# Band sums in two row halves behind the scores, the next query product behind them, and five of eight band groups normalized earlier

## The chip, the cores and the metric

The kernel runs on one core of a Trainium2 chip. The metric is device microseconds (us) of one execution, lower is better; before the change the median of three runs is 2634.23 us (2633.81 to 2636.1).

A core has five engines that run side by side and meet through semaphores: TensorE (PE in the profile; PEld is its weight load), VectorE (DVE), ScalarE (ACT), GpSimd (POOL) and SyncE (SP, which here issues transfers). Each engine takes its instructions in the order in which the program lists them. Matmuls write to PSUM, eight banks of 512 fp32 columns on 128 partitions.

## The reference

One layer over x of shape (2, 256, 128, 128), that is B, T, F, C, all fp32: attention along T with a causal mask, attention along F with a band mask, then a feed-forward layer, each with a layer norm before it and a residual after it.

```python
cm = _causal_mask(x.shape[1])
bm = _band_mask(x.shape[2], BAND)          # |i - j| <= 16 of 128
xt = _ln(x, ln_t_w, ln_t_b).transpose(0, 2, 1, 3)
x = x + _mha(xt, t_wi, ..., H_T, cm).transpose(0, 2, 1, 3)
xf = _ln(x, ln_f_w, ln_f_b)
x = x + _mha(xf, f_wi, ..., H_F, bm)       # 4 heads of 32
xn = _ln(x, ln_n_w, ln_n_b)
h = jax.nn.gelu(xn @ w1.T + b1, approximate=False)   # 128 -> 512 -> 128
x = x + (h @ w2.T + b2)
```

## The kernel before, in words

The work is cut into groups of 512 tokens (`NT` = 4 tiles of 128). First come 128 groups of attention over time (`OverTime`), which end some 930 us into the program. Then follow 16 runs; each has 8 groups of band attention (`OverBands`) and then the 8 feed-forward groups (`FeedForward`) on the same tokens. Everything is unrolled, and every instruction on the main path is kept in program order (`InOrder`, whose one line, L907, is the line of nearly all rows of the profile). So the order in which `run` (L1275) calls the groups' methods is the order on each engine.

`run` is a pipeline: in step n it works on group n and its neighbours. In the steps of a run I count the band groups 0 to 7, and call "step n" the one whose scores are those of band group n. There, before the change, TensorE does in this order:

- scores of n: per tile and half of the keys, 4 heads, 64 keys by 80 queries (only queries that can lie in the band);
- sums of n-1: for each head the column sums of the weights, as a product of a block of ones with all 128 keys, 512 queries;
- weigh of n-1: values times weights; output of n-2: the out projection;
- queries, keys, then values of n+1.

ScalarE does in the step: exponentials of the four heads of n (`pf`), logarithm and exponential that make a first inverse of the sums of n-1 (`ln`, `r`), then copies of queries, keys and values of n+1 (`qT`, `kT`, `v`). VectorE does: clamp and band of the fourth head of n (`bank<-bank,band`), normalization and transposition of group n+3 (`xh`, `z`; the result goes to DRAM as `turned` and comes back as `xnT`), the residual of n-2 (`x<-bank,x`, which empties the out projection's bank), and a correction step of the inverse with the division of n-1 (`bank<-bank,r`, `u`, `oT`). In some steps it also does the layer norm's statistics of a later group (`stats`, `mv`). GpSimd masks the other three heads (`pf<-pf`, six instructions) and makes the roots (`rstd`).

The last steps of a band run overlap with the first feed-forward steps. A feed-forward step is two hidden products, the second product of the group before (`w2T_sb,hT`, 64 products of 128 columns), and two more hidden products.

PSUM banks are handed out in rotation (`turn_of_bank`, L943): a product that is written to a bank waits until the reader of the bank's last content is done.

## Time and profile before

| what | value |
|---|---|
| median of 3 runs | 2634.23 us |
| span of the profiled execution | 2631.9 us |
| PE busy | 2617.8 us (99%) |
| DVE busy | 2140.8 us (81%) |
| ACT busy | 1838.8 us (70%) |
| POOL busy | 1958.6 us (74%) |
| in a stretch of band steps (1459.70 to 1507.00): PE, DVE, ACT, POOL | 47.30, 40.81, 38.22, 31.45 of 47.30 us |
| in the feed-forward steps behind it (1507.00 to 1565.50) | 58.50, 44.46, 25.16, 38.43 of 58.50 us |

The span goes from the first to the last instruction of one profiled execution; its own total time is not given apart from that, and the span stands 2.3 us under the median of the runs. In the rows of the timeline a row gives the start, the time from the first start to the last end, the engine, the line, the operation, what it writes and reads, and the count. A fp32 matmul appears as two records. Since matmuls are pipelined, the time of a block on TensorE is read from its start to the start of the next block, not from the second column.

### The profile page before, as it was taken

The numbers are of one execution on the slowest core, as the hardware profiler recorded it, in microseconds if no ns is written. First come the engines' busy times: TensorE is split into PE (matmuls) and PEld (weight loads), VectorE is DVE, ScalarE is ACT, GpSimd is POOL, SyncE is SP. The second block draws the span as 40 slices with busy tenths as digits, with TensorE's granted clock in tenths as the row PEclk, the third lists the DMA queues.
The fourth block names the chain that finished last, engine by engine and source line by source line (L and its number), as shares of the span: only waits on it lengthen the run. The fifth ranks groups of instructions, "written<-read, shape, count | busy, mean of one in ns | idle before, by whom it ended". The sixth has DMA issues, their size and how long they took to land.

```text
span 2631.9 us, 156460 instructions
## 1 busy us (share of the span) xinstructions
PE 2617.8 (99%) x68688; PEld 1837.4 (70%) x68688; DVE 2140.8 (81%) x6410; ACT 1838.8 (70%) x3543; POOL 1958.6 (74%) x2311
## 2 busy tenths in 40 slices
PE   9999999999999999999999999999999999999999
PEld 6666666666766767666777776667676677777776
DVE  8888888888888887977878779788797797887974
ACT  7989988999899875564655746647557466475573
POOL 7999999999999987666667666665776666757762
PEclk9999999999999999999999999999999999999999
DMA  6656555565565454445454544554454445554543
GB/s 155 167 149 158 149 149 149 155 155 149 149 158 149 122 127 119 115 123 127 118 124 124 123 122 117 126 128 120 122 126 120 120 119 131 123 120 123 123 104 88
DMA packets 469797, 344.97 MB, mean 131 GB/s; under 512 B 43120, under 2 KB 404464, under 8 KB 469104
## 3 DMA queue, kind: packets, MB, share of 16 engines
q1 hardware_dynamic: 468408, 334.41, 50.5%
q8 instruction: 540, 8.85, 1.5%
q14 instruction: 153, 1.25, 0.2%
q10 hardware_dynamic: 696, 0.46, 0.1%
HBM read 167.98 MB, written 166.72 MB: 127 GB/s over the span
## 4 chain that ended last, share of the span: by engine, by line
PE 99%; DVE 0%; issue 0%; DMA 0%; ACT 0%; ACTq 0%; DVEq 0%
PE bank L907 99%; DMA x<-in_x 0%; DVE xh L907 0%; DVE bank L907 0%; DVE res L907 0%; DVE stats L907 0%; DVE oT L907 0%; DVE u L907 0%; DVE xnT L907 0%; ACTq L907 0%; ACT p L907 0%; DVE vy L907 0%; ACT lnv L907 0%; DVE mv L907 0%; ACT root L907 0%
## 5 line engine op out<-in xcount | busy, mean ns | idle before, releaser
L907 ACT ACTIVATE hT<-bank,b 128x512 f32<-128x512 f32 x512 | 348.1, 688 | 524.2 <-PE bank L907 483.2
L907 POOL TENSOR_SCALAR_AFFINE_SELECT pf<-pf 128x512 f32<-128x512 f32 x768 | 477.7, 637 | 185.3 <-ACT pf L907 159.1
L907 PEld LDWEIGHTS bank<-w2T_sb,hT 128*32 128x32 f32 x16384 | 467.4, 110 | 54.8 <-issue 29.0
L907 PE MATMUL bank<-xnT,wf 128*32 128x512 f32 x4096 | 492.4, 592 | 0.5 <-DVE xnT L907 0.5
L907 PE MATMUL bank<-xnT,w1f 128*32 128x512 f32 x4096 | 486.3, 592 | 0.2 <-issue 0.2
L907 PE MATMUL bank<-w2T_sb,hT 128*32 128x128 f32 x16384 | 482.8, 273 | 1.0 <-issue 1.0
L907 ACT ACTIVATE p<-bank 128x512 f32<-128x512 f32 (+1 forms) x1024 | 430.6, 494 | 62.9 <-PE bank L907 62.9
L907 DVE TENSOR_SCALAR xh<-x,mv,rstd 128x160 f32<-128x160 f32 (+1 forms) x1012 | 394.3, 432 | 59.7 <-POOL rstd L907 49.4
L907 POOL TENSOR_SCALAR_AFFINE_SELECT p<-p 128x1024 f32<-128x1024 f32 (+2 forms) x384 | 364.5, 949 | 57.5 <-ACT p L907 49.1
L907 PEld LDWEIGHTS bank<-wf,xnT 128*32 128x32 f32 x8192 | 243.3, 110 | 144.1 <-issue 101.6
L907 POOL TENSOR_TENSOR p<-p,p 128x512 f32<-128x512 f32 x256 | 324.6, 1291 | 10.6
L907 DVE BATCH_NORM_STATS2 stats<-x 128x6 f32<-128x128 f32 x1536 | 329.0, 276 | 3.4 <-DMA x<-in_x 3.4
L907 POOL TENSOR_SCALAR rstd<-mv 128x4 f32<-128x4 f32 x251 | 57.8, 230 | 361.7 <-DVE mv L907 360.5
L907 PEld LDWEIGHTS bank<-xnT,w1f 128*32 128x32 f32 x4096 | 183.6, 110 | 171.6 <-issue 109.6
L907 PE MATMUL bank<-qT,kT 32*64 32x80 f32 (+4 forms) x16384 | 302.0, 271 | 0.1
L907 PEld LDWEIGHTS bank<-qT,kT 32*64 32x64 f32 x16384 | 260.0, 131 | 51.2 <-ACT kT L907 50.6
L907 DVE TENSOR_TENSOR res<-bank,res 128x512 f32<-128x512 f32 (+1 forms) x259 | 170.3, 658 | 153.3 <-PE bank L907 144.7
L907 ACT ACTIVATE pf<-bank 128x512 f32<-128x512 f32 x512 | 265.8, 602 | 35.5 <-PE bank L907 31.3
L907 PE MATMUL bank<-wn,oT 128*32 128x128 f32 x8192 | 283.8, 274 | 0.1
L907 DVE STREAM_TRANSPOSE z<-xh 128x512 f32<-128x512 f32 x380 | 270.3, 711 | 13.3
L907 PE MATMUL bank<-wf,xnT 128*32 128x128 f32 x8192 | 276.5, 273 | 0.0
L907 POOL TENSOR_TENSOR rstd<-rstd,mhalf 128x4 f32<-128x4 f32 x251 | 260.8, 1039 | 20.9
(100 smaller groups left out, 3820.3 us busy)
## 6 DMA issues: line engine op xcount, KB each, us to landing
turned<-z SPq DMA_DIRECT2D x1520, 64.0 KB, 2.7
xnT<-turned SPq DMA_DIRECT2D x380, 256.0 KB, 3.2
x<-res SPq DMA_DIRECT2D x256, 128.0 KB, 2.5
x<-x SPq DMA_DIRECT2D x128, 256.0 KB, 4.1
out<-res SPq DMA_DIRECT2D x252, 128.0 KB, 2.3
x<-in_x SPq DMA_DIRECT2D x124, 256.0 KB, 4.3
x<-in_x SPq DMA_DIRECT2D x4, 128.0 KB, 2.8
x<-in_x SPq DMA_DIRECT2D x6, 64.0 KB, 2.9
```

The costliest lines, as they stand in the source:

```text
L907: return self.tc.keep_in_program_order(emit(*args, **kwargs))
```

## The change

- The sums of a band group n-1, in the steps in which n is a band group too, are made in two parts right behind the scores of n. Of 128 queries of a tile, the first 48 can only have weights on the first 64 keys, and the last 48 on the last 64 keys. The outer part sums these over 64 rows each, into two banks (`rp` and `lower`); the middle part sums the 32 queries between over all 128 rows. The logarithm and the first multiplication then work on two pieces.
- The queries' product of n+1 stands right behind the sums, ahead of the weighing; the copy of the queries stands behind the inverse.
- The residual of n-2 stands inside the division of n-1, behind its first multiplication.
- Band groups 3 to 7 of every run but the first are normalized and transposed three steps earlier than before, beside another group: 3, 4 and 5 in the last three feed-forward steps of the run before, 6 and 7 in the steps of bands 0 and 1. Bands 5 to 7 then normalize feed-forward groups as before, bands 2 to 4 nothing.
- Statistics and root of the first feed-forward groups stand behind the masks of their step, statistics on VectorE thus right behind the clamp.
- In feed-forward steps the hidden products of n stand between the halves of the second product of n-1, and the stores of results are issued one step later, from ScalarE's queue.
- Banks are taken from a list in the order in which they were given back.

The diff, cut to its core:

```diff
+EDGE = HALF - BAND
@@ class Attention
-    def divide(self):
+    def divide(self, between=None):
...
-        vector.tensor_tensor(self.rp, self.rp, self.r0, ALU.mult)
+        self.multiply()
+        if between is not None:
+            between()
         u = path.work.tile([P, NT * P], F32, name="u", bufs=2)
         vector.scalar_tensor_tensor(u, self.rp, 2.0, self.r0, ALU.subtract, ALU.mult)
@@ class OverBands
+    def outer_sums(self):
+        self.split = True
+        self.rp = self.take("rp", [P, NT * P])
+        self.lower = self.take("lower", [P, NT * EDGE])
+        for h in range(H):
+            self.sums_of(h, in_tiles(self.rp)[:, :, 0:EDGE], slice(0, EDGE), slice(0, HALF))
+            self.sums_of(h, in_tiles(self.lower), slice(P - EDGE, P), slice(HALF, P))
+
+    def middle_sums(self):
+        q = slice(EDGE, P - EDGE)
+        for h in range(H):
+            self.sums_of(h, in_tiles(self.rp)[:, :, q], q, slice(0, P))
+
+    def sums_of(self, h, to, q, rows):
+        self.path.tensor.matmul(
+            to[rows_of(h)], self.path.k.ones[rows, 0:D], self.p[rows, h, :, q],
+            start=True, stop=True, skip_group_check=True,
+        )
+
+    def invert(self):
...
+        path.scalar.activation(in_tiles(ln)[:, :, 0 : P - EDGE], in_tiles(self.rp)[:, :, 0 : P - EDGE], AF.Ln)
+        path.scalar.activation(in_tiles(ln)[:, :, P - EDGE : P], in_tiles(self.lower), AF.Ln)
...
+    def multiply(self):
...
+        vector.tensor_tensor(rp[:, :, low], in_tiles(self.lower), r0[:, :, low], ALU.mult)
+        self.give("lower")
+        vector.tensor_tensor(rp[:, :, q], rp[:, :, q], r0[:, :, q], ALU.mult)
@@ class FeedForward
+    def weigh_around(self, other):
+        self.zp = self.take("zp", [P, NT, P])
+        self.weigh_tiles(range(0, 2))
+        other.hidden((2,))
+        self.weigh_tiles(range(2, NT))
+        other.hidden((3,))
@@ class BoundedPath
+    def release(self, i):
+        if i in self.free:
+            self.free.remove(i)
+        self.free.append(i)
@@ run
         def statistics_of_feed(n):
-            if n + 5 in early:
-                do(n + 5, "statistics")
             if at(n + 4, FeedForward) and n + 4 not in early:
                 do(n + 4, "statistics", "root")
+        def turn_ahead(n):
+            for i in (n + 3, n + 6):
+                ahead = at(n + 3, OverBands) and at(i, OverBands) and i not in run0
+                if not at(i, OverTime) and (i == n + 3 or ahead) and not at_turn(i):
+                    do(i, "normalize", "turn")
...
-            if n + 4 in early:
-                do(n + 4, "root")
             do(n, "first_half", "first_function", "first_mask")
+            if n + 4 in early:
+                do(n + 4, "statistics", "root")
...
+            self.storing = self.scalar if feeds[2] and n < len(groups) - NT else self.sync
+            do_at(n - 2, FeedForward, "put")
...
-            do_at(n + 3, (OverBands, FeedForward), "normalize", "turn")
+            turn_ahead(n)
...
-            do(n - 1, "weigh")
+            self.two_parts = bands[2]
+            if bands[2]:
+                do(n - 1, "sums")
+            if bands[2] and bands[3]:
+                do(n + 1, "queries")
+            if feeds[1] and feeds[2]:
+                groups[n - 1].weigh_around(groups[n])
+            else:
+                do(n - 1, "weigh")
             do(n - 1, "invert_exactly" if turn else "invert")
+            if bands[2] and bands[3]:
+                do(n + 1, "take_query")
...
-            do(n - 1, "divide")
+            if bands[1] and bands[2]:
+                groups[n - 1].keep = True
+                groups[n - 1].divide(partial(do, n - 2, "finish"))
+            else:
+                do(n - 1, "divide")
...
-            do_at(n + 1, OverBands, "queries_keys", "take_query", "take_key")
+            if bands[2] and bands[3]:
+                do(n + 1, "keys", "take_key")
+            else:
+                do_at(n + 1, OverBands, "queries_keys", "take_query", "take_key")
```

Three places in the order of the instructions matter for what follows. A row names what is written and read and the output's shape; the number behind `bank` tells the eight banks apart (108 to 115). The first is TensorE in a band step between the scores of n (`qT,kT`) and those of n+1: sums (`pf,ones`), weigh (`pf,v`), output (`wn`,`oT`), then queries and keys (`xnT,wf`) and values (`wf,xnT`). Before:

```order
L907 MATMUL bank_113<-qT,kT 64x80
L907 MATMUL bank_108<-pf,ones 32x512 x4
L907 MATMUL bank_109<-pf,v 32x128 x16
L907 MATMUL bank_114<-wn_241,oT 32x128 x16
L907 MATMUL bank_115<-xnT,wf_238 32x512 x4
L907 MATMUL bank_110<-xnT,wf_238 32x512 x4
L907 MATMUL bank_111<-wf_238,xnT 32x128 x16
```

and of the change:

```order
L1031 MATMUL bank_115<-pf,ones 32x192
L1031 MATMUL bank_108<-pf,ones 32x4x32 x4
L1031 MATMUL bank_114<-xnT,wf_238 32x512 x4
L1031 MATMUL bank_110<-pf,v 32x128 x16
L1031 MATMUL bank_113<-wn_241,oT 32x128 x16
L1031 MATMUL bank_111<-xnT,wf_238 32x512 x4
L1031 MATMUL bank_109<-wf_238,xnT 32x128 x16
L1031 MATMUL bank_112<-qT,kT 64x80
L1031 MATMUL bank_114<-qT,kT 64x80
L1031 MATMUL bank_115<-qT,kT 64x80
L1031 MATMUL bank_113<-qT,kT 64x80
```

The first row of the change is the last of the eight outer products (four of 32x4x48 into bank 108 alternate with four of 32x192 into bank 115). Queries moved up to stand behind the sums. The last four rows are the four heads' scores of n+1: the fourth head goes to bank 113, into which the out projection of n-2 was written in the same step, and the third to bank 115, which held `lower`.

The second place is VectorE in a band step with statistics. Before, from one clamp to the next:

```order
L907 SCALAR_TENSOR_TENSOR bank_113<-bank_113,band 128x512
L907 TENSOR_SCALAR xh<-x,mv,rstd 128x5x32 x4
L907 STREAM_TRANSPOSE z<-xh 128x512
L907 TENSOR_TENSOR x_27227<-bank_114,x_27227 128x512
L907 TENSOR_TENSOR bank_108<-bank_108,r_29670 128x512
L907 SCALAR_TENSOR_TENSOR u<-bank_108,r_29670 128x512
L907 TENSOR_TENSOR oT<-bank_109,u 128x4x4x32
L907 BN_STATS stats<-x_27227 128x6 x4
L907 BN_AGGR mv<-stats 128x2 x4
```

and of the change, in the steps of bands 5 and 6:

```order
L1031 SCALAR_TENSOR_TENSOR bank_112<-bank_112,band 128x512
L1031 BN_STATS stats<-x_27483 128x6 x4
L1031 BN_AGGR mv<-stats 128x2 x4
L1031 TENSOR_SCALAR xh<-x_27483,mv,rstd 128x5x32 x4
L1031 STREAM_TRANSPOSE z<-xh 128x512
L1031 TENSOR_TENSOR bank_115<-bank_109,r_30151 128x4x48
L1031 TENSOR_TENSOR bank_115<-bank_115,r_30151 128x4x80
L1031 TENSOR_TENSOR x_27483<-bank_113,x_27483 128x512
L1031 SCALAR_TENSOR_TENSOR u<-bank_115,r_30151 128x512
L1031 TENSOR_TENSOR oT<-bank_114,u 128x4x4x32
```

The statistics moved from behind the division to right behind the clamp, and the residual (`x<-bank`) moved behind the two multiplications. Before, the steps of bands 3, 4 and 5 have statistics, and all eight steps have the normalization (`xh`, `z`). Now bands 4, 5 and 6 have statistics and bands 2, 3 and 4 have no normalization, so both meet in the steps of bands 5 and 6.

The third place is ScalarE in a band step, from the last exponential of n to the copy of the values of n+1. Before:

```order
L907 ACTIVATE pf<-bank_115 128x512
L907 ACTIVATE ln<-bank_110 128x512
L907 ACTIVATE r_50758<-ln 128x512
L907 ACTIVATE qT<-bank_109,bq_283 128x512
L907 COPY kT<-bank_112 128x512
L907 COPY v<-bank_113 128x512
```

and of the change:

```order
L1031 ACTIVATE pf<-bank_113 128x512
L1031 ACTIVATE ln<-bank_114 128x4x80
L1031 ACTIVATE ln<-bank_109 128x4x48
L1031 ACTIVATE r_51929<-ln 128x512
L1031 ACTIVATE qT<-bank_111,bq_283 128x512
L1031 COPY kT<-bank_108 128x512
L1031 COPY v<-bank_115 128x512
```

The order of the steps is the same; the logarithm became two instructions. The product that `qT` copies is now ready earlier.

More of the change, by code (lines that the diff above doesn't have):

```diff
@@ L380, in __init__, with take, give @@
         self.before, self.store = before, store
+        self.taken = {}
+    def take(self, name, shape, i=None):
+        free = self.path.free
+        if i is None:
+            i = free[0]
+        if i in free:
+            free.remove(i)
+        self.taken[name] = i
+        return self.path.bank(shape, name, i)
+    def give(self, *names):
+        for name in names:
+            if name in self.taken:
+                self.path.release(self.taken.pop(name))
     def load(self):
@@ L569, in bias, with queries, keys, queries_keys @@
         )
-    def queries_keys(self):
+    def queries(self):
+        path = self.path
+        self.qp = self.take("qp", [P, NT * P], self.place.get("qp"))
+        product(path, self.qp, path.k.wf[self.which][:, 0:P], self.xnT)
+    def keys(self):
         path = self.path
         wf = path.k.wf[self.which]
-        self.qp = path.bank([P, NT * P], "qp", self.place.get("qp", path.held.pop("qp", None)))
-        product(path, self.qp, wf[:, 0:P], self.xnT)
-        self.kp = path.bank([P, NT * P], "kp", self.place.get("kp"))
+        self.kp = self.take("kp", [P, NT * P], self.place.get("kp"))
         product(path, self.kp, wf[:, P : 2 * P], self.xnT)
+    def queries_keys(self):
+        self.queries()
+        self.keys()
     def take_query(self):
@@ L663, in values @@
         wv = path.k.wf[self.which][:, 2 * P : 3 * P]
-        self.vp = [path.bank([P, 2, P], "vp", self.place.get(f"vp{s}")) for s in range(2)]
+        self.vp = [self.take(f"vp{s}", [P, 2, P], self.place.get(f"vp{s}")) for s in range(2)]
         for i in range(NT):
@@ L679, in first_tiles @@
         self.p0 = path.work.tile([P, 2, H, 2 * P], F32, name="p0", tag="p", bufs=3)
-        self.s0 = {h: path.bank([P, 2, 2 * P], "sp", path.banks[f"a{h}"]) for h in range(H)}
+        self.s0 = {h: self.take(f"s0{h}", [P, 2, 2 * P], path.banks[f"a{h}"]) for h in range(H)}
     def second_tiles(self):
@@ L685, in second_tiles @@
         self.p1 = path.work.tile([P, 2, H, 2, P], F32, name="p1", tag="h", bufs=2)
[L686 removed]
+        self.s1 = {h: self.take(f"s1{h}", [P, 2, P], path.banks[f"b{h}"]) for h in range(H)}
     def first_scores(self, h, s, e):
@@ L728, in weigh @@
         path, v = self.path, self.v
-        rp = path.bank([P, 2, 2, P], "rp", self.place.get("rp"))
+        rp = self.take("rp", [P, 2, 2, P], self.place.get("rp"))
         for n in range(2):
@@ L771 @@
     which = 1
-    follow = ("yp",)
     by_vector = 1
+    split = False
+    rp = None
     def scores(self, heads):
         path = self.path
-        self.sp = {h: path.bank([P, NT * P], "sp") for h in heads}
+        self.sp = {h: self.take(f"sp{h}", [P, NT * P]) for h in heads}
         for i in range(NT):
@@ L823, in weigh @@
             )
-        self.op = path.bank([P, NT * P], "op")
+    def weigh(self):
+        path = self.path
+        if self.rp is None:
+            self.sums()
+        self.op = self.take("op", [P, NT * P])
         for i in range(NT):
@@ L867, in second_function, with weigh_tiles @@
         self.gelus((2, 3))
+    def weigh_tiles(self, tiles):
+        path, NI = self.path, self.path.k.NI
+        for i in tiles:
+            for j in range(NI):
+                product(
+                    path, self.zp[:, i], self.hT[:, j, i * P : (i + 1) * P], path.k.w2T[:, j, :],
+                    start=(j == 0), stop=(j == NI - 1),
+                )
+    def weigh_around(self, other):
[4 more added lines that the diff above has]
+        other.hidden((3,))
     def weigh(self):
@@ L871, in weigh @@
         if self.last:
-            zp = [path.bank([P, P], "zp") for i in range(NT)]
+            zp = [self.take(f"zp{i}", [P, P]) for i in range(NT)]
         else:
-            self.zp = path.bank([P, NT, P], "zp")
+            self.zp = self.take("zp", [P, NT, P])
             zp = [self.zp[:, i] for i in range(NT)]
@@ L1288, in do_at @@
                 do(n, *names)
-        for i in range(len(groups) - 2):
-            if at(i, OverBands) and at(i + 1, OverBands):
-                groups[i].follow = ("yp", "qp")
         run0 = [i for i in range(len(groups)) if at(i, OverBands)][: RUN // NT]
@@ L1412, in run @@
                 statistics_of_feed(n)
-            if not turn:
+            if feeds[1] and feeds[2]:
+                do(n, "second_function")
+            elif not turn:
                 do(n, "second_half", "second_function")
```

96 lines of the change are left out of this document (72 added, 24 removed).

## The prediction

> **What bounds the kernel now.** I read the page first, for which engine the end hangs on:
>
> ```profile
> span 2631.9 us, 156460 instructions
> PE 2617.8 (99%) x68688; PEld 1837.4 (70%) x68688; DVE 2140.8 (81%) x6410; ACT 1838.8 (70%) x3543; POOL 1958.6 (74%) x2311
> PE 99%; DVE 0%; issue 0%; DMA 0%; ACT 0%; ACTq 0%; DVEq 0%
> ```
>
> TensorE is busy nearly always and is nearly the whole chain. So time is won by less TensorE work or by fewer hidden pauses, and lost wherever TensorE newly waits. A busy PE can hide pauses, so next I took the timeline and read block starts. One band step, scores to scores:
>
> ```profile
> 1497.43 0.97 PE L907 MATMUL bank<-qT,kT 32*64 32x80 f32 x64
> 1498.33 1.06 PE L907 MATMUL bank<-pf,ones 128*32 128x512 f32 x8
> 1499.21 1.06 PE L907 MATMUL bank<-pf,v 128*32 128x128 f32 x32
> 1500.08 1.06 PE L907 MATMUL bank<-wn,oT 128*32 128x128 f32 x32
> 1500.95 1.90 PE L907 MATMUL bank<-xnT,wf 128*32 128x512 f32 x16
> 1502.67 1.06 PE L907 MATMUL bank<-wf,xnT 128*32 128x128 f32 x32
> 1503.66 0.97 PE L907 MATMUL bank<-qT,kT 32*64 32x80 f32 x64
> ```
>
> A step lasts 6.23 us: scores 0.90, sums 0.88, weigh 0.87, output 0.87, queries and keys 1.72, values 0.99. How much is pause? The starts and ends of runs tell:
>
> ```profile
> 925.92 0.97 PE L907 MATMUL bank<-qT,kT 32*64 32x80 f32 x64
> ...
> 1459.73 0.96 PE L907 MATMUL bank<-qT,kT 32*64 32x80 f32 x64
> 1478.43 0.96 PE L907 MATMUL bank<-qT,kT 32*64 32x80 f32 x64
> 1491.20 0.97 PE L907 MATMUL bank<-qT,kT 32*64 32x80 f32 x64
> 1565.44 0.97 PE L907 MATMUL bank<-qT,kT 32*64 32x80 f32 x64
> 1599.81 0.64 PE L907 MATMUL bank<-pf,v 128*32 128x128 f32 x16 [0.30 <-issue]
> 2624.28 1.49 PE L907 MATMUL bank<-w2T_sb,hT 128*32 128x128 f32 x48
> ```
>
> From the first band scores (925.92) to the end of the last product (2625.77) are 1699.9 us for 16 runs. The run from 1459.73 to 1565.44 took 105.7; two of its steps (1478.43 to 1491.20) took 12.77, 0.31 over twice 6.23, so a clean run is 105.4. All 16 clean would be 1686, so pauses cost some 13.5 us. They look like the row at 1599.81: in the middle of a block, on nobody ("issue").
>
> **The sums.** Eight records of 512 columns, four side by side, take 0.88 us: 0.86 ns a column. The scores are 64 records of 80 columns; one after another they would take 4.4 us, four abreast 1.1, and they take 0.90. So row tiles do run side by side, about eight abreast where none waits. Two parts need two passes of 192 columns (0.33 us, eight abreast) and two of 128 (0.22), together 0.55. But the shape of the tiles changes once more in each step (scores 32 by 64, outer 64 by 32, then 128 by 32). The values' block takes 0.99 against 0.87 for the same 32 records of 128 columns in weigh: 0.12 for a change of shape. I take 0.55 + 0.12 + 0.01 for a slow start = 0.68, a gain of 0.20 a step. Ends: 0.55 if no change costs anything; 1.00 if the two row halves run in turn.
>
> [...]
>
> There are seven such steps a run, bands 1 to 7. Whether TensorE can use the 0.20 is set by what else ends late there.
>
> **The steps of bands 5 and 6: VectorE.** The fourth head's scores of n+1 now go into the bank that the residual of n-2 empties, and VectorE does that residual after everything else up to the multiplication. The prices, from a step with statistics, and from one in which VectorE had waited for the scores:
>
> ```profile
> 1479.58 0.70 DVE L907 SCALAR_TENSOR_TENSOR bank<-bank,band 128x512 f32<-128x512 f32 x1 [0.64 <-PE bank L907]
> ...
> 1486.15 0.67 DVE L907 SCALAR_TENSOR_TENSOR bank<-bank,band 128x512 f32<-128x512 f32 x1
> 1486.73 1.60 DVE L907 TENSOR_SCALAR xh<-x,mv,rstd 128x160 f32<-128x160 f32 x4
> 1488.37 0.71 DVE L907 STREAM_TRANSPOSE z<-xh 128x512 f32<-128x512 f32 x1
> 1489.00 0.65 DVE L907 TENSOR_TENSOR x<-bank,x 128x512 f32<-128x512 f32 x1
> 1489.58 0.69 DVE L907 TENSOR_TENSOR bank<-bank,r 128x512 f32<-128x512 f32 x1
> 1490.30 0.69 DVE L907 SCALAR_TENSOR_TENSOR u<-bank,r 128x512 f32<-128x512 f32 x1
> 1491.02 0.69 DVE L907 TENSOR_TENSOR oT<-bank,u 128x512 f32<-128x512 f32 x1
> 1491.63 0.86 DVE L907 BATCH_NORM_STATS2 stats<-x 128x6 f32<-128x128 f32 x4
> 1492.41 0.36 DVE L907 BATCH_NORM_AGGREGATE mv<-stats 128x2 f32<-128x6 f32 x4
> 1492.69 0.67 DVE L907 SCALAR_TENSOR_TENSOR bank<-bank,band 128x512 f32<-128x512 f32 x1
> ```
>
> The clamp can start 1.15 us after the scores (1479.58 less 1478.43). This step kept VectorE busy for 6.54 us, more than TensorE's 6.23; before, the excess fell on later work. In the new order, from the start of the scores: 1.15, clamp 0.58, statistics 1.06, normalization 1.64, transposition 0.63, so 5.06. Then two multiplications in place of one. The prices of whole and half:
>
> ```profile
> L907 DVE TENSOR_TENSOR bank<-bank,r 128x512 f32<-128x512 f32 x240 | 166.8, 695 | 102.1 <-PE bank L907 78.9 <-ACT r L907 23.2
> L907 DVE TENSOR_TENSOR orow<-bank,rows_sb 128x256 f32<-128x256 f32 x1 | 0.4, 423 | 0.0
> ```
>
> That is 1.06 ns a column and 0.15 fixed, so 0.36 and 0.49 for 192 and 320 columns; with handovers 0.90. The residual takes 0.65: its end is at 6.61, and TensorE goes on at about 6.65, though it could at 6.03. The rest of VectorE's step (0.72, 0.61) delays the next clamp by 0.07, so step 6 lasts 6.72. Against 6.23 before: +0.42 and +0.49. Nothing covers this: behind the fourth head stand the whole sums, queries and weighing. Ends: no loss at all, if something lets the residual go earlier; 0.1 more each if handovers add up.
>
> **Step 1, and the chain of the other steps: ScalarE.** In the step of band 1 there is no output product, and ScalarE runs without a pause:
>
> ```profile
> 1466.85 0.97 PE L907 MATMUL bank<-qT,kT 32*64 32x80 f32 x64
> 1467.86 2.07 ACT L907 ACTIVATE pf<-bank 128x512 f32<-128x512 f32 x4 [0.29 <-PE bank L907]
> 1469.79 0.63 ACT L907 ACTIVATE ln<-bank 128x512 f32<-128x512 f32 x1
> 1470.45 0.63 ACT L907 ACTIVATE r<-ln 128x512 f32<-128x512 f32 x1
> 1470.99 0.67 ACT L907 ACTIVATE qT<-bank,bq 128x512 f32<-128x512 f32 x1
> 1471.11 0.70 DVE L907 TENSOR_TENSOR bank<-bank,r 128x512 f32<-128x512 f32 x1 [0.15 <-ACT r L907]
> 1471.56 0.58 ACT L907 COPY kT<-bank 128x512 f32<-128x512 f32 x1
> 1472.20 0.97 PE L907 MATMUL bank<-qT,kT 32*64 32x80 f32 x64
> ```
>
> The keys' copy ends at 1472.14, the next scores start at 1472.20: 5.35 us is ScalarE's chain as well as TensorE's work. So the step keeps its length whatever the sums save, and the logarithm in two pieces adds to it. A second instruction costs between nothing (overlap) and 0.3; I take 0.05, as the columns stay the same and the first piece's start is hidden by the exponentials. Step 1: +0.05.
>
> In steps 2, 3, 4 and 7 the multiplication starts 4.26 (1471.11 less 1466.85) + 0.05 after the scores; + 0.90 + 0.65 + 0.05 is 5.91, under TensorE's 6.03. So they gain the full 0.20 each, with 0.1 to spare; in step 7 no scores follow. The early queries make their copy start right after `r`; they give room, not time.
>
> **What is moved without a term.** The normalizations moved to the last feed-forward steps cost VectorE 2.27 each there; such a step then holds two of them, 0.65 and 1.06: 6.25 us, under the step's 6.9 (64 products at 0.87 per 16, four hidden products at 0.86). Their eight transfers go out on SP three steps ahead. Masks take GpSimd six instructions, and standing ahead of the roots they come earlier. The stores on ScalarE's queue wait for nothing, being one step late. Uncovered, any of these would be one wait of under 1 us a run.
>
> **The sum.** Per run: 0.05 (step 1), four times -0.20, +0.42, +0.49 = +0.16; by 16 runs +2.6 us. Of the 13.5 us of pauses I count off some 7: what fell into steps 5 and 6, where TensorE now waits for VectorE anyway (they are 12 of 105 us, but hold more than their share of pauses, an estimate of 5), and 2 for fewer transfers beside the band steps. Together -4. The profiled span would go from 2631.9 to 2628, and the median, 2.3 above the span, from 2634.2 to **2630**. About 0.2% (5 us) is what a measurement here tells from no change; this forecast lies just inside.
>
> **The rivals.**
> - *VectorE does not hold steps 5 and 6* (another bank falls free, or the clamp comes earlier). For: in the step from 1486.15 an equal load on VectorE did not stop TensorE. Against: there the residual stood ahead of the multiplication. Then six steps gain 0.20: -1.15 a run, -18, with pauses -4: 2612.
> - *The row halves run in turn* and the two parts do not shorten the sums: 1.00 a step. For: no row shows tiles of 64 by 32. Against: the scores' eight abreast. Steps 1 to 4 and 7 then lose 0.12 each: 0.60 + 0.91 = 1.5 a run, +24, less 7: 2651.
> - *The chain through ScalarE takes TensorE's place, so it is slower.* It decides from the point at which the second logarithm costs over 0.15: at 0.3 the residual ends at 6.15, the four light steps gain 0.08 and step 1 loses 0.3: 0.3 - 0.32 + 0.91 = +0.89, +14, less 7: 2641. For: the 5.35 of step 1 has no slack. Against: the four exponentials are through in 1.93 (1467.86 to 1469.79), 0.48 each, with 512 columns; instructions that don't wait for each other overlap.
>
> **How the numbers follow.** Forecast 0.50 (its own range 2622 to 2638: the sums at 0.62 to 0.78, pauses off by 5), VectorE not holding 0.20, halves in turn 0.13, ScalarE's chain 0.12, anything else 0.05. Faster by over 0.2%: 0.4 of the forecast and the whole first rival, 0.42. Slower by over 0.2%: the second rival, most of the third, a little of the forecast and the rest, 0.25. Within 0.2%: 0.33. The range 2608 to 2648 leaves out the second rival and the edge of the first.
>
> **What would show it.** From scores to outer sums to queries 0.68 us; light steps 6.03; step 1 at 5.40; steps 5 and 6 at 6.65 and 6.72, with the residual `x<-bank,x` ending just before the fourth head's scores start; VectorE without idle time in them. Sums over 0.88, or steps 5 and 6 of 6.03, would each make the forecast wrong, to the slow and the fast side.

## The result, and the profile after

The kernel after took **2659.79 us** (median of four, 2659.58 to 2668.31), beside 2635.16 us before (2633.81 to 2637.4): a ratio of **1.0106, interval 1.0095 to 1.0118**. So it is 25 us slower, where 2630 was forecast and 2608 to 2648 was the range. The profiled execution is the longest of the four, 8.5 us over the median, so readings that sum pauses over it may be too large by up to that much.

The page of the kernel after, its span, its TensorE and the chain that ended last, and the queue that brings TensorE's instructions (packets, MB, share of the 16 engines):

```profile
span 2666.4 us, 160431 instructions
PE 2624.3 (98%) x70480; PEld 1795.2 (67%) x70480; DVE 2157.6 (81%) x6522; ACT 1827.8 (69%) x3655; POOL 1956.5 (73%) x2311
q8 instruction: 555, 9.09, 1.5%
PE 81%; DVE 11%; ACT 3%; issue 2%; DMA 2%; POOL 0%; SPq 0%; ACTq 0%; DVEq 0%; POOLq 0%
```

TensorE was 99% of the chain before; now VectorE holds 11% of it and "issue" 2%. The queue's 555 packets are 16.4 KB each. TensorE has 70480 products and as many weight loads, 140960 instructions. What a packet holds shows where almost nothing but TensorE's instructions differs: beside the kernel before (137376 of them, 540 packets), the quarters of experiment 6 have 149664 and 588 packets, the whole array of experiment 13 has 122016 and 480. That is 256 instructions for each packet more or less, both times, while the other instruction queue (q14) has 153 packets in all three. 140960 are then 551 packets of the 555, so this queue is nearly all TensorE's; that will matter.

A light step of the kernel after, scores to scores, from the timeline (start, length, engine, line):

```profile
2565.87 0.97 PE L1031 MATMUL bank<-qT,kT 32*64 32x80 f32 x64
2566.76 0.91 PE L1031 MATMUL bank<-pf,ones 64*32 64x192 f32 x24
2567.49 1.04 PE L1031 MATMUL bank<-xnT,wf 128*32 128x512 f32 x8
2568.35 1.06 PE L1031 MATMUL bank<-pf,v 128*32 128x128 f32 x32
2569.22 1.06 PE L1031 MATMUL bank<-wn,oT 128*32 128x128 f32 x32
2570.10 1.04 PE L1031 MATMUL bank<-xnT,wf 128*32 128x512 f32 x8
2570.95 1.06 PE L1031 MATMUL bank<-wf,xnT 128*32 128x128 f32 x32
2571.94 0.97 PE L1031 MATMUL bank<-qT,kT 32*64 32x80 f32 x64
```

The sums take 0.73 us (2566.76 to 2567.49) instead of 0.88, and the step 6.07 instead of 6.23. The change does on TensorE what it was taken to do. What it lost is seen in the starts of the runs, here the first and the last of the kernel after:

```profile
925.25 0.97 PE L1031 MATMUL bank<-qT,kT 32*64 32x80 f32 x64
2553.35 0.97 PE L1031 MATMUL bank<-qT,kT 32*64 32x80 f32 x64
```

and the last of the kernel before (its first started at 925.92):

```profile
2519.04 0.97 PE L907 MATMUL bank<-qT,kT 32*64 32x80 f32 x64
```

Fifteen runs took 1628.1 us, 108.5 each; before 1593.1, 106.2 each. In the table "step n" goes from the scores of n to those of n+1, the lengths are clean ones, read from runs in which the step shows no pause, and the last column is the mean run:

| | step 0 | 1 | 2, 3, 4, 5 | 6 | 7 and feed-forward | clean run | mean run |
|---|---|---|---|---|---|---|---|
| before | 7.12 | 5.36 | 6.23 | 6.23 | 61.78 | 105.4 | 106.2 |
| after | 7.12 | 5.40 | 6.08 | 6.46 | 62.62 | 105.9 | 108.5 |

Clean is not common everywhere. In the kernel after, step 3 lasts 6.08 us in only two of the 16 runs, and its median is 7.1. Of the stretches behind step 7, 61.78 stands in two of the fifteen runs of the kernel before, and 61.71 and 61.94 in four each. So the difference of the clean runs is known to about 0.1 us.

There are two losses: the clean run is some 0.5 us longer (8 us over 16 runs), and what lies over it, mostly pauses, grew from 0.8 to 2.6 us a run (13 to 42 us in this profile; up to 9 less at the median). The idle time of TensorE itself in the band and feed-forward part (from 925 us on: what was waited for, us in total, times, longest), after:

```profile
PE bank L1031 <- issue: 19.8, 27, 2.0
PE bank L1031 <- DVE oT L1031: 4.2, 11, 0.5
PE bank L1031 <- DVE x L1031: 3.0, 14, 0.2
```

and before:

```profile
PE bank L907 <- issue: 2.7, 7, 0.8
```

Most of it is on nobody. One such pause, in the step of band 3 of the twelfth run:

```profile
2134.68 0.97 PE L1031 MATMUL bank<-qT,kT 32*64 32x80 f32 x64
2135.57 0.53 PE L1031 MATMUL bank<-pf,ones 64*32 64x192 f32 x9
2138.08 1.44 PE L1031 MATMUL bank<-pf,ones 64*32 64x192 f32 x15 [1.98 <-issue]
2139.29 1.94 PE L1031 MATMUL bank<-xnT,wf 128*32 128x512 f32 x8
```

TensorE stops in the middle of a block, with nine of its 24 products done, waits for no semaphore, and goes on 2 us later. In the transfers of the same stretch a packet of the instruction queue comes 5.7 us after the one before it, and TensorE goes on 1.5 us behind its end. A row shows less than its pause costs: these sums last 3.72 us (2135.57 to 2139.29) instead of 0.73.

That this is the rule and not one case shows in the count of TensorE's records (products, weight loads and those of its sequencer). Counted from the program's first, all 27 pauses on nobody of the kernel after and all 7 of the kernel before stand 193 or 194 records past a multiple of 256, so always a whole number of packets apart, and TensorE goes on 1.2 to 1.6 us behind the end of a packet. In the experiments below it is the same (193 to 195; 1.2 to 1.7 us). So the pauses on nobody are waits for the next packet of instructions.

### The profile page after: what moved, and what is told of

Same layout as the page of the kernel before. It is cut to its first block, busy times and chain, and to the rows that moved or that the text cites. A ratio compares the mean times of both kernels' runs of the same rounds, so it can differ in the third digit from the quotient of the medians.

```text
span 2666.4 us, 160431 instructions
## 1 busy us (share of the span) xinstructions
PE 2624.3 (98%) x70480; PEld 1795.2 (67%) x70480; DVE 2157.6 (81%) x6522; ACT 1827.8 (69%) x3655; POOL 1956.5 (73%) x2311
## 4 chain that ended last, share of the span: by engine, by line
PE 81%; DVE 11%; ACT 3%; issue 2%; DMA 2%; POOL 0%; SPq 0%; ACTq 0%; DVEq 0%; POOLq 0%
PE bank L1031 81%; DVE xh L1031 2%; DVE bank L1031 2%; ACT pf L1031 1%; DVE ln L1031 1%; DVE stats L1031 1%; DVE x L1031 1%; DMA xnT<-turned 1%; DVE oT L1031 1%; DVE u L1031 1%; DMA turned<-z 1%; DVE z L1031 1%; ACT r L1031 1%; DVE mv L1031 0%; ACT ln L1031 0%
## 5 line engine op out<-in xcount | busy, mean ns | idle before, releaser
L1031 ACT ACTIVATE hT<-bank,b 128x512 f32<-128x512 f32 x512 | 342.3, 688 | 537.0 <-PE bank L1031 378.1
L1031 PEld LDWEIGHTS bank<-w2T_sb,hT 128*32 128x32 f32 x16384 | 461.2, 110 | 142.8 <-issue 117.3
L1031 PE MATMUL bank<-xnT,wf 128*32 128x512 f32 x4096 | 513.3, 594 | 2.2 <-issue 0.7
L1031 PE MATMUL bank<-w2T_sb,hT 128*32 128x128 f32 x16384 | 495.7, 273 | 1.2 <-ACT hT L1031 0.6
L1031 PE MATMUL bank<-xnT,w1f 128*32 128x512 f32 x4096 | 493.9, 592 | 0.1
L1031 DVE TENSOR_TENSOR bank<-bank,r 128x192 f32<-128x192 f32 (+1 forms) x352 | 185.2, 526 | 207.2 <-ACT r L1031 122.6
L1031 PE MATMUL bank<-qT,kT 32*64 32x80 f32 (+4 forms) x16384 | 315.8, 272 | 11.8 <-issue 6.0
L1031 PEld LDWEIGHTS bank<-qT,kT 32*64 32x64 f32 x16384 | 266.7, 131 | 70.5 <-ACT kT L1031 52.1
L1031 PEld LDWEIGHTS bank<-wn,oT 128*32 128x32 f32 x8192 | 221.0, 110 | 39.7 <-DVE oT L1031 16.9
```

The costliest lines, as they stand in the source:

```text
L1031: return self.tc.keep_in_program_order(emit(*args, **kwargs))
```

## The experiments

Two theories of the pauses stood at the start. **T**: the data transfers that the change packs more closely delay the fetch of TensorE's instructions. **D**: the two-part sums add 32 instructions to each step (200 products and as many weight loads, 400, instead of 368) and shorten it, and the fetch does not keep up (some expectations call this F, and its rival, that the short dense stretch or its shapes make the pauses, S). For the clean run the theory was that **VectorE's load** in the steps with statistics makes its loss.

**1. The sums alone.** Everything else of the change is taken back:

```diff
-            for i in (n + 3, n + 6):
+            for i in (n + 3,):
-            self.storing = self.scalar if feeds[2] and n < len(groups) - NT else self.sync
+            self.storing = self.sync
...
-                groups[n - 1].divide(partial(do, n - 2, "finish"))
+                groups[n - 1].divide()
```

> The change with everything but the sums in two parts taken back: queries, normalizations, statistics, roots, residual, stores and the feed-forward order stand as in the kernel before (only the banks come from the change's free list). Both theories: sums 0.73 us, steps 2 to 7 at 6.08 (six times -0.15 a run, -14 us over 16 runs), step 1 5.40 (+1), the stretch behind step 7 back at 61.9. Theory T (transfers): TensorE's pauses without a semaphore come from the data transfers that the change packs closely, so they stay near before's 2.7 us: 2622. Theory D (density): they come from the dense stretch of scores and 96-column sums, which asks for more instructions in less time than before, so they stay near the change's 20 us: 2639.

2660.2 us, ratio 1.0105 (1.0088 to 1.0122): the sums alone lose as much as the whole change. Its idle time on TensorE, the pauses that no semaphore explains:

```profile
PE bank L1031 <- issue: 16.6, 27, 1.5
PE bank L1031 <- POOL pf L1031: 2.8, 13, 0.8
```

This speaks for D. Of the 21 us over its expectation some 8 lie behind step 7 (62.4 us in the mean instead of 61.9), and a part is the second row, a wait for masks that D did not have (see 8); the rest was not taken apart.

**2. All but the sums.**

```diff
-            self.two_parts = bands[2]
+            self.two_parts = False
```

> The change with the sums in one part again (eight records of 512 columns), all else as in the change. Sums 0.88, light steps 6.23 (four times +0.15 a run, +10 us), the two heavy steps as in the change. Theory T (the packed transfers delay the instruction fetch): pauses without a semaphore stay near 20 us, 2670. Theory D (density of the two-part sums): they fall to about 3 us, 2652.

2637.7 us, 1.0013 (1.0003 to 1.0022), with

```profile
PE bank L1031 <- issue: 3.7, 7, 1.1
```

So the queries, normalizations, statistics, stores and the feed-forward order together cost 3.7 us, and the two-part sums on top of them 22. Without the sums, even the two heavy steps cost next to nothing: scores to scores 6.23 and 6.25.

**3. and 4. No normalization ahead; stores on SP as before.**

```diff
-            for i in (n + 3, n + 6):
+            for i in (n + 3,):
```

> The change with each group's normalization three steps ahead again, none six steps ahead. Now three steps (4, 5, 6) hold statistics and normalization on VectorE: one heavy step more, +0.4 a run, +6 us; the transfers of the normalizations are spread over the run again. Theory T: the pauses of step 3 go, 15 us less: 2651. Theory D: they stay: 2666. The stretch behind step 7: stays near 63 if it comes from the roots and statistics behind the masks, goes to 62 if it comes from the normalizations moved into the last feed-forward steps.

```diff
-            self.storing = self.scalar if feeds[2] and n < len(groups) - NT else self.sync
+            self.storing = self.sync
-        for group in groups[-NT:]:
+        for group in groups:
             group.prompt = True
```

> The change with each store right behind its residual and on SP's queue again, as before. SP then waits for each residual before it sends the next load, so the loads and stores don't go out together. Theory T: pauses without a semaphore fall, by half or more: 2650 or below. Theory D: no difference, 2660.

2666.94 us (1.0129, 1.0112 to 1.0146) and 2658.95 us (1.0099, 1.0070 to 1.0127), the pauses on nobody 16.8 and 19.1 us. So T falls as what makes the sum of the pauses. But the transfers bear on where they fall: in the change 13.3 of the 19.8 us on nobody lie in step 3, without normalizations ahead they are spread over steps 2 to 7. Steps 2, 3 and 5 of the twelfth run of the kernel after, in the windows view (us, PE busy and products, granted clock, share of the transfer engines, GB/s):

```profile
2128.60:2134.68 6.08, 6.08 (x205) 1.00 0.81 199
2134.68:2144.70 10.02, 8.04 (x205) 0.83 0.29 63
2150.77:2156.85 6.08, 6.08 (x205) 1.00 0.04 10
```

Step 3 comes right behind the step with the most transfers, and step 5, with the fewest, has no pause on nobody in any run, though it asks for as many instructions. In the band steps of the change the packets of instructions stand 3.8 us apart in the quarter of cases with the least transfers and 4.5 us in the quarter with the most. These go together in time; no run tested them by themselves. The granted clock of 0.83 goes with this one pause; around the other 26 of the change it is 1.00. The stretch behind step 7 (62.9 in the mean) is not from the normalizations either.

**5. and 6. As many instructions, elsewhere.** In the kernel before, the queries' and keys' products are cut into halves, then into quarters; no two-part sums.

```diff
-        product(path, self.qp, wf[:, 0:P], self.xnT)
+        m = NT * P // (2 if self.which else 1)
+        for c in range(0, NT * P, m):
+            product(path, self.qp[:, c : c + m], wf[:, 0:P], self.xnT[:, c : c + m])
```

> The kernel before with the frequency queries' and keys' products each cut into two halves of 256 columns: the same columns and the same time on TensorE, 32 instructions more in each band step (400 in 6.23 us instead of 368), as many as the two-part sums add, but spread over the 1.72 us in which TensorE has the fewest. No row tile, no other order. Theory F (the fetch of TensorE's instructions cannot deliver much more than 256 in 3.4 to 3.9 us, whatever stretch they are in): it now pauses as in the change, 8 to 17 us without a semaphore, 2640 to 2650. Theory S (the short, dense stretch of scores and two-part sums, or the shape of its tiles, makes the pauses): none, 2634.

> The same with four quarters of 128 columns: 464 instructions a band step, 74 in a us at 6.23. Theory F: TensorE is held to the fetch's pace in the band steps; at 3.5 to 3.9 us for each 256, a step takes 6.3 to 7.1 us: 2650 to 2720, and the length of a step gives the pace. Theory S: 2634 to 2640.

2647.48 us (1.0050, 1.0033 to 1.0067) and **2727.22 us (1.0356, 1.0339 to 1.0374)**. The columns are as before, and with halves so is the clean step (6.24). Halves:

```profile
PE bank L911 <- issue: 8.7, 13, 2.0
```

Quarters, the same row, then steps 1 to 6 of the eleventh run in the windows view and the instruction queue's packets there:

```profile
PE bank L911 <- issue: 51.9, 84, 2.0
...
2060.37:2102.89 42.52, 40.01 (x1377) 1.00 0.48 119
...
q8 instruction: 11, 0.18, 2.0%
```

1377 products with their weight loads are 2754 instructions in 42.52 us: 64.8 in a us, 256 in 3.95 us, and eleven packets of 256 came in that time. The queue is busy 2% of the 16 engines' time, so it does not fill them. TensorE got about 65 instructions in a us here; a second such window (1045.13 to 1088.40, 1408 products) gives 65.1, and the fifteen runs 62 to 69. Single packets come closer together than 3.95 us: two start 3.33 us apart at the least in the band and feed-forward part of the kernel before, and 2.17 in that of the kernel after. The 93 us that the kernel is slower are nearly twice the row of 51.9. The two-part sums ask for 400 in 6.08 us, 66 in a us; before it was 368 in 6.23, 59.

**7. Every second step.** The sums alone, in two parts in steps 2, 4 and 6 only.

```diff
-            self.two_parts = bands[2]
+            self.two_parts = bands[2] and (n - run0[0]) % 2 == 0
```

> The sums alone in two parts (as in the first experiment), but only in the steps of bands 2, 4 and 6: 62 instructions in a us on average instead of 66. Three steps a run save 0.15, -7 us at most. Theory F: the pauses fall from 16.6 us to 3 to 8; the stretch behind step 7 stays near 62.0: 2632 to 2640. Theory S: half of the pauses stay, 8 us, and the wait for the masks too: 2646.

2643.18 us (1.0037, 1.0025 to 1.0048), 3 us over the range of F; 6.0 us on nobody, as F has it with 62 instructions in a us. A part of the rest is the wait for masks, in step 6 and behind the scores of 7 (6.6 us on the weight loads, 2.0 before).

**8. The masks.** In the first experiment the weight loads of the sums waited for GpSimd's masks 22 times (10.8 us in total, before 8 times and 2.0): in one part the sums read head after head, in two parts the outer products of all heads come first. Here statistics and roots stand behind the masks again, as in the change:

```diff
-            if n + 4 in early:
-                do(n + 4, "root")
             do(n, "first_half", "first_function", "first_mask")
+            if n + 4 in early:
+                do(n + 4, "statistics", "root")
```

> The sums alone in two parts (as in the first experiment), but with the statistics and roots of the three first feed-forward groups one step later and behind the masks, as in the change. The two-part sums read the masked weights of all four heads 0.4 us earlier; here GpSimd has them ready. The wait of the sums for the masks (0.39 us a run) goes: 2660 - 6 = 2654. If what it saves only moves to the instruction fetch or to VectorE: 2660.

2666.36 us (1.0122, 1.0105 to 1.0139). The weight loads of this kernel:

```profile
PEld bank L1031 <- DVE oT L1031: 22.7, 16, 1.9
```

and of the first experiment:

```profile
PEld bank L1031 <- DVE oT L1031: 15.6, 16, 1.1
PEld bank L1031 <- POOL pf L1031: 10.8, 22, 1.2
```

The time is over both expectations. The wait for the masks goes (to 1.7), but the one for `oT` grows in the turn, the steps in which a band run passes into its feed-forward groups, and the stretch behind step 7 from 62.4 to 63.0. A reading of it is that late roots make late normalizations, and these a late division; that chain was not tested by itself.

**9. to 11. Statistics and roots.** First as before, then (a part of the computation left out) replaced by a constant, in the change and in the second experiment.

```diff
+            if n + 5 in early:
+                do(n + 5, "statistics")
...
             if n + 4 in early:
-                do(n + 4, "statistics", "root")
+                do(n + 4, "root")
```

> The change with the statistics of the three first feed-forward groups one step earlier and their roots ahead of the masks again, as before. One step (band 5) holds statistics and normalization instead of two: -0.4 a run, -6 us. If the roots behind the masks make the stretch behind step 7 longer, it goes from 62.8 to 62.0, -11 us, less 0.3 us a run for masks that now end after the sums want them: 2646. If the instruction fetch sets the pace of the band steps, the time won in them comes back as pauses: 2655.

```diff
         self.mv = self.means()
+        if self.known:
+            vector.memset(self.mv, 1.0)
+            return
```

> The change with the statistics of the three first feed-forward groups of each run left out (a constant is written in their place, the root and the normalization go on with it; a part of the computation is missing). VectorE has 1.0 us less in the steps of bands 4, 5 and 6. If TensorE's waits behind the heavy steps and in the turn to the feed-forward groups come from VectorE's load, they go, 1 us a run: the stretch behind step 7 falls from 62.8 to 62.0 and the time to 2642 to 2648 (a part may come back as fetch pauses). If they come from the roots standing behind the masks, nothing changes: 2659.

> The same with the sums in one part (the second experiment without these statistics). If the 3.7 us that the second experiment had over the kernel before are VectorE's load at the turn (0.25 a run): 2634. Otherwise 2638.

2657.44 (1.0087, 1.0071 to 1.0104); 2651.86 (1.0076, 1.0057 to 1.0096); 2633.31 (0.9998, 0.9988 to 1.0007). With the statistics gone the clean step 6 falls from 6.46 to 6.08 and the stretch behind step 7 from 62.62 to 62.10: 0.9 us a run, 14 us, of which 8 arrive; the pauses on nobody stay (17.5). With the statistics moved back only 0.3 to 0.4 behind step 7 is won, and 2.4 us in all, for which the two intervals overlap. So VectorE's load of statistics is what the clean run pays for: without it it is 105.0, under the 105.4 of before. This takes away work that the kernel before does too, so it prices the load and not its place; the place of statistics and roots alone is worth little. The last of the three, with whole sums and no such load, is level with the kernel before.

**12. to 15. Fewer instructions.** Queries, keys, values and output of the bands as products of the whole 128 by 128 array (one product for four, 120 instructions less in a step), in the change, in the kernel before, and in the change with statistics or residual moved back.

```diff
+    if whole:
+        path.tensor.matmul(out, weights, x, start=start, stop=stop)
+        return
```

> The change with the queries', keys', values' and output products of the bands as products of the whole 128 by 128 array instead of four 128 by 32 tiles each: the same columns, but 120 instructions less in a band step (282 instead of 402), one change of the tiles' shape more (about 0.12 a step). Theory F (the fetch's pace): the pauses without a semaphore go from 20 us to under 3; light steps 6.20, heavy ones and the stretch behind step 7 as in the change: 2660 - 25 + 12 = 2647. If the pauses belong to the two-part sums themselves and not to the count of instructions, they stay: 2672.

> The same edit in the kernel before: 248 instructions in a band step instead of 368. Steps 6.35 instead of 6.23 for the change of shape (+13 us over 112 steps). Theory F: the pauses spread over its band steps (some 13 us by the runs' lengths) go: 2634. Otherwise they stay: 2647.

> The same edit in the change with statistics and roots where they stood before. With the fetch out of the way this shows the waits alone: one heavy step instead of two (-0.4 a run) and the stretch behind step 7 by 0.3 to 0.7 a run shorter: 8 to 16 us under the first of these four. If the statistics and roots don't matter: the same as that.

The fourth of them has this besides:

```diff
-                if not inner:
-                    do(n - 2, "finish")
+                do(n - 2, "finish")
...
-                groups[n - 1].divide(partial(do, n - 2, "finish"))
+                groups[n - 1].divide()
```

> The same edit in the change with the residual of n-2 ahead of the multiplications again. If the heavy steps are set by the residual behind the multiplications (the gate of the fourth head's scores), they shrink by 0.4 each and the time is 10 us under the first of these four, as far as the division that now ends later doesn't hold the next output product; if VectorE's total load sets them, nothing is won.

2686.03 us (1.0197, 1.0180 to 1.0214), 2668.18 (1.0123, 1.0106 to 1.0140), 2684.83 (1.0190, 1.0173 to 1.0207), 2684.26 (1.0191, 1.0174 to 1.0208). One step of the kernel before with this edit:

```profile
2131.62 0.97 PE L910 MATMUL bank<-qT,kT 32*64 32x80 f32 x64
2132.52 1.07 PE L910 MATMUL bank<-pf,ones 128*32 128x512 f32 x8
2133.40 1.06 PE L910 MATMUL bank<-pf,v 128*32 128x128 f32 x32
2134.39 1.16 PE L910 MATMUL bank<-wn,oT 128*128 128x128 f32 x8
2135.38 1.88 PE L910 MATMUL bank<-xnT,wf 128*128 128x512 f32 x4
2137.10 1.05 PE L910 MATMUL bank<-wf,xnT 128*128 128x128 f32 x8
2138.09 0.97 PE L910 MATMUL bank<-qT,kT 32*64 32x80 f32 x64
```

and its idle time on TensorE:

```profile
PE bank L910 <- issue: 0.4, 2, 0.2
```

The pauses are all but gone: from the second run on, each of its steps 2 to 6 lasts 6.46 us, in every run. In the change they are all 6.64, with no row on nobody at all. By the starts of the runs the mean run is 0.2 us over the clean one instead of 0.8, and in the change 0.1 instead of 2.6. But no time is won: the step is 0.23 longer (0.12 each in the blocks of weigh and output), in the change 0.56. The whole array costs more than the one change of shape that was expected. With TensorE that slow it also covers VectorE, so 14 and 15 did not tell the statistics or the residual apart: steps 2 to 6 are 6.64 in all three.

**16. The start of a run.** In the kernel before, the feed-forward product in the step of band 0 (474 instructions in 7.12 us) as a product of the whole array.

```diff
+            if at(i, FeedForward) and at(i + 1, OverBands):
+                groups[i].whole = True
...
-                start=(j == 0), stop=(j == NI - 1),
+                start=(j == 0), stop=(j == NI - 1), whole=self.whole,
```

> The kernel before with the second product of the last feed-forward group ahead of each run of bands (it is issued in the step of band 0) as products of the whole 128 by 128 array: 282 instructions instead of 474 in that step, two changes of shape a run (0.24, +4 us). If instructions fetched ahead are a reserve that this step uses up (474 in 7.12 us is 67 in a us), the later steps of the run now pause less, by 4 to 9 us: 2629 to 2634. If there is no such reserve: 2638.

2636.19 us, 1.0006 (0.9996 to 1.0015), 2.5 us on nobody as before. The step itself is 0.27 longer, 4 us over the runs, and the time grew by 2.6, so a small gain elsewhere is not excluded, but no reserve that this step uses up shows. The packets say the same: in the kernel before, at 335 of 345 places where the instructions of one packet give way to the next, the packet after that had not landed. So the fetch was seldom more than one packet ahead there, and one late packet can be enough for a pause, as in the one at 2138.08 above.

**17. and 18. The two-part sums with fewer instructions around them.** Keys and values as products of the whole array in the change (with the statistics of before); queries, keys and values in the sums alone.

```diff
-        product(path, self.kp, wf[:, P : 2 * P], self.xnT)
+        product(path, self.kp, wf[:, P : 2 * P], self.xnT, whole=self.which == 1)
```

> The change with the statistics and roots of before, and with the keys' and values' products of the bands, which stand side by side ahead of the scores, as products of the whole array: 60 instructions less in a band step (342), one change of shape more (0.12). If the fetch's pace is what the two-part sums ran into: steps of 6.20 without pauses, the stretch behind step 7 62.4 to 62.6: 2630 to 2636, at or under the kernel before. If whole-array products cost more than that one change each (as the fourth last to last experiments had it: 0.23 a step), 2640 to 2645.

> The sums alone in two parts, as in the first experiment, with queries, keys and values as products of the whole array (330 instructions a step), again one change of shape more: steps of 6.20 without pauses, the wait of the sums for the masks stays (0.3 a run or less, as TensorE comes later): 2630 to 2636. If each block of the whole array costs 0.1 more: 2645.

2647.49 us (1.0052, 1.0038 to 1.0065) and 2656.47 (1.0077, 1.0063 to 1.0092), both over their expectations. Against experiment 9, which differs by this edit alone, the first is 10 us faster, though its clean steps went from 6.08 to 6.29. It pauses little:

```profile
PE bank L1034 <- issue: 1.5, 3, 0.6
```

The price of the whole array shows in the second: queries and keys 1.82 us instead of 1.72, beside 0.12 for the shape in the output block ahead of them (0.99 instead of 0.87). In the step shown under 12 to 15, where output ahead of them is in the whole array too, queries and keys take 1.72: the extra falls on the first block behind the change of shape.

```profile
2128.32 1.06 PE L1034 MATMUL bank<-wn,oT 128*32 128x128 f32 x32
2129.31 1.98 PE L1034 MATMUL bank<-xnT,wf 128*128 128x512 f32 x4
2131.13 1.05 PE L1034 MATMUL bank<-wf,xnT 128*128 128x128 f32 x8
```

It still waits for masks (5.3 us on the weight loads) and for `oT` (16.3). No complete version found beats the kernel before.

Ordered by the instructions that the clean step asks for in a us, the pauses on nobody:

| kernel | instructions, us | in a us | on nobody, us |
|---|---|---|---|
| before, whole array | 248, 6.46 | 38 | 0.4 |
| change, whole array | 280, 6.64 | 42 | none listed |
| sums alone, whole queries, keys, values | 328, 6.29 | 52 | 5.5 |
| change, whole keys and values | 340, 6.29 | 54 | 1.5 |
| before | 368, 6.23 | 59 | 2.7 |
| all but the sums | 368, 6.23 | 59 | 3.7 |
| sums in every second step | 384, 6.15 | 62 | 6.0 |
| before, halves | 400, 6.24 | 64 | 8.7 |
| sums alone | 400, 6.08 | 66 | 16.6 |
| change | 400, 6.08 | 66 | 19.8 |
| before, quarters | 464, 6.23 | 74 | 51.9 |

One row, the third, is out of order, and is not explained.

## Why the prediction was wrong

- **The sums**: 0.68 forecast, 0.73 measured; light steps 6.03 forecast, 6.08 measured. The row halves do run side by side, so that rival falls. Right, but a quarter of the gain did not come. The "about eight abreast" did not follow from the scores, whose 4.4 us of columns in 0.90 us are about five abreast; the sums come near it (0.73 us less 0.22 for the middle part and 0.12 for the shape leaves 0.39 for the outer part, an estimate; 0.33 at eight abreast).
- **Step 1**: 5.40 forecast, 5.40 measured where it is clean; ScalarE's chain did not take over. From the first logarithm to the exponential behind it (`r`) it is 0.73 us in the median of the 112 steps with two pieces, and 0.66 with one piece before: 0.07 for the second instruction, where 0.05 was taken.
- **Steps 5 and 6**: the mechanism was right. The fourth head's scores wait for the residual behind VectorE's work. TensorE of the kernel after in the last run:

```profile
2590.17 1.35 PE L1031 MATMUL bank<-qT,kT 32*64 32x80 f32 x64
2591.45 0.91 PE L1031 MATMUL bank<-pf,ones 64*32 64x192 f32 x24
...
2596.71 1.42 PE L1031 MATMUL bank<-qT,kT 32*64 32x80 f32 x64
2598.06 0.35 PE L1031 MATMUL bank<-pf,ones 64*32 64x192 f32 x1
```

  and VectorE between its clamps:

```profile
2591.79 0.69 DVE L1031 SCALAR_TENSOR_TENSOR bank<-bank,band 128x512 f32<-128x512 f32 x1
...
2595.70 0.87 DVE L1031 TENSOR_TENSOR bank<-bank,r 128x192 f32<-128x192 f32 x2
2596.47 0.68 DVE L1031 TENSOR_TENSOR x<-bank,x 128x512 f32<-128x512 f32 x1
...
2598.39 0.69 DVE L1031 SCALAR_TENSOR_TENSOR bank<-bank,band 128x512 f32<-128x512 f32 x1
```

  The scores' blocks take 1.28 and 1.35 us instead of 0.90 and end behind the residual, which ends at 2597.15; VectorE has no idle time in 6.60 us. From the end of one scores block to the next, step 5 is 6.46 (2584.99 to 2591.45) and step 6 is 6.61 (2591.45 to 2598.06); 6.65 and 6.72 were forecast. So the two steps lose 0.61 us a run, not 0.91. The two multiplications take 0.77 (2595.70 to 2596.47) instead of 0.90.
- **What was moved without a term**: wrong here. Behind step 7 the prediction had only the sums' gain; the stretch is 62.62 instead of 61.78. The delay of scores 7 (0.45 in the rows above, 0.52 in most runs) belongs to the step before; the rest is the division in the turn, in the eleventh run:

```profile
2069.04 1.04 PE L1031 MATMUL bank<-xnT,w1f 128*32 128x512 f32 x8
2070.50 1.08 PE L1031 MATMUL bank<-wn,oT 128*32 128x128 f32 x32 [0.42 <-DVE oT L1031]
```

  The hidden product of 2069.04 needs 0.86, so output could have started at 2069.90; it waits 0.6 for `oT`. Over the kernel the weight loads wait 20.0 us for `oT`, 9.9 before. VectorE comes out of step 6 without a gap, and time that TensorE saves in the band steps it gives back in the turn. In all the clean run grew by some 0.5 us instead of the 0.16 forecast, 8 us instead of 2.6. That alone would have stayed inside the range.
- **The pauses are the step that failed.** The prediction read the pauses "on nobody" as something to count down by 7 us, of it 2 "for fewer transfers beside the band steps". They grew by 17 us or more in the profile (19.8 beside 2.7 us in the rows, from 13 to 42 by the runs' lengths). Their sum does not hang on the data transfers (experiments 3, 4) but on how many instructions TensorE asks for in a us (1, 2, 5, 6, 12 to 15), and each stands where a packet of instructions ends. No run shows the 2 us for fewer transfers. The 5 us for steps 5 and 6 can be read as come true, as the kernel after has no pause on nobody there; more than twice as much was lost in step 3 (13.3 us). The working counted the added instructions' columns and shapes, and never the instructions. The page before had shown both sides: TensorE with 68688 products at 59 instructions in a us in the band steps, and pauses of 0.30 us in the middle of blocks.

The pauses on nobody go with what is asked for: 0.4 us or no row at 38 to 42 instructions in a us, 1.5 to 5.5 us at 52 to 59, 16.6 and 19.8 at 66; asked for 74, TensorE got 256 in 3.95 us.

Open stay whether the transfers of step 2 are what puts the pauses into step 3 when normalizations go ahead, how VectorE's load and the roots share the turn's 0.8 us a run, and what sets the pace of the packets.

## What to carry to other kernels

Where an engine works through many small tiles, count its instructions in a us of each stage beside its columns; an edit that saves time by cutting one product into three can be lost to the fetch of instructions, as here (0.15 us won in a clean step, 22 us lost in all), and pauses on nobody in the middle of a block were its sign (19.8 us beside 2.7). Whether they are the fetch's, the count of the engine's records tells: here each stood at the same place in 256. Measure what the fetch brings in a us once, by cutting a product into pieces without changing anything else. When TensorE gets shorter in a step where another engine is busy without a gap, follow the gain to the next place where the two meet: here it was given back there (0.8 us a run behind step 7).

## What was not expected of the hardware

Asked for 74 instructions in a us, TensorE got about 65 (2754 in 42.52 us), at a granted clock of 1.00 and with its instruction queue at 2.0% of the transfer engines; pauses on nobody show below that too, 1.5 to 5.5 us at 52 to 59. They stood 256 records apart or a multiple of it, 1.2 to 1.7 us behind the end of a packet of instructions. A change from tiles of 128 by 32 to the whole array cost 0.12 us in the block ahead of it (weigh 0.99 instead of 0.87) and 0.10 to 0.12 in the first block behind it (queries and keys 1.82 instead of 1.72), and nothing in the blocks after that (1.72). The row halves of the sums do run side by side: 24 records, 16 of 192 columns and 8 of 128, and the change of shape in 0.73 us, where eight records of 512 columns took 0.88.
